# A macaron block as one stream of tile steps, with the state space stage spread over them

## The chip, the cores and the metric

The kernel runs on one core of one Trainium2 chip. The metric is the device time of one execution in microseconds (us). A core has five engines that work side by side, each strictly in the order of its own instructions: TensorE (PE, matmuls; its weight loads are shown apart as PEld), VectorE (DVE), ScalarE (ACT), GpSimd (POOL) and SyncE (SP), which here issues all transfers. They wait for one another by semaphores. SBUF is the working memory with 128 partitions; PSUM, with eight banks of 512 float32 per partition, takes TensorE's results.

## The reference, cut to what matters

x is 2048 tokens of 128 features. A transformer F of six layers is applied twice, with the same weights, around a state space layer S:

```python
x = x + 0.5 * F(layernorm(x))
x = x + S(layernorm(x))
x = x + 0.5 * F(layernorm(x))
...
# a layer of F; shift_tokens moves the upper half of the features by one token
x = attn_layer(shift_tokens(x), Wqkv[i], q_scale[i], k_scale[i], Wo[i]) + x
x = ffn_layer(shift_tokens(x), ln_g[i], ln_b[i], W1[i], b1[i], W2[i], b2[i]) + x
...
# in S: 256 channels with 16 states each, token after token
s = dA_t * s + dBu_t
y = jnp.einsum('bdn,bn->bd', s, C_t)
```

Attention is local: 16 heads of 64, windows of 32 tokens, and each window sees itself and the window before. The queries and keys are normalised and rotated. The feed-forward part has 341 hidden features and a gated GELU. So a token of F depends on tokens shortly before it, never on later ones, and S carries 256 x 16 states from the first token to the last.

## The kernel before, in words

All is float32, and the features lie on the partitions. The program has three stages one after the other: `transformer(k, xt, False)`, `state_space(k, xt)`, `transformer(k, xt, True)`.

**A transformer** runs over 6 x 16 tiles of 128 tokens. A tile's work is cut into some fifty short pieces, each on one engine. `run` loops over the steps i; in a step it goes through the list ORDER of (piece, lag) and emits piece by piece for tile i - lag. So the work of up to eight tiles stands interleaved in each engine's queue, in an order written out by hand (`manual_schedule`; SP is not in it). The pieces of a tile, with their lines:

- `project` (L263): queries and keys, two matmuls of 512 columns each; ScalarE squares them (L275), VectorE multiplies with cosines (L281) and sines (L287), GpSimd adds (L296), sums (L302) and a few short instructions give the norms, GpSimd scales (L328).
- `turn` (L341): 16 transposes; ScalarE copies them out (L350, L355).
- `score` (L378 masks, L389): 64 small matmuls; then copy (L400), maximum (L405), subtraction (L411), exponent (L417), sum (L422), division (L427), and a 32x32 transpose on VectorE (L437).
- `average` (L470): with the tile's inputs (transposed by L444, shifted by two copies between partitions on SP, L459 to L461) as weights, into two wide PSUM buffers z; ScalarE copies both into one tile zt of 4 x 16 x 32 columns (L482).
- `mix` (L490): the value and output weights were merged beforehand into one 128x128 matrix m per head. So the output of a tile is 16 matmuls, one per head, each with 128 columns (4 windows of 32), summed in one PSUM bank:

```python
for h in range(HEADS):
    self.nc.tensor.matmul(
        out=st.y_ps.rearrange("p (b q) -> p b q", q=WIN),
        lhsT=self.w[g // NT].m[:, h // 2, h % 2, :],
        rhs=st.zt[:, :, h, :],
```

- `residual` (L500) adds it to the stream r0 and writes r1.

Every fourth tile the feed-forward part follows for a block of 512 tokens: centring (L512), squares, variance (L534), reciprocal root, gates and values (L562), GELU (L581), product (L593), contraction (L606), residual (L617). Every layer's weights are loaded ahead by `load`; in the first pass `merge` (L207) forms m, and `biases` (L229) multiplies W1 with the bias of the norm: 12 records with one moving column.

PSUM is shared by three wide buffers of two banks (tag w: x_ps, t_ps, s_ps, z_ps and two thirds of g and a) and two narrow ones of one bank (tag n: the transposed inputs, centring, variance, mix, contraction, a third of g and a). A buffer goes to the next user in the order of the program; the writer waits until its last reader is done.

**The state space stage** is scheduled by the framework, not by hand. Per block of 512 tokens: two norms (L130, L88, L108, L120), projections (L772, L777), convolution (L783, L792), parameters (L803), and for the whole sequence the step sizes delta (L820 to L838). Then per block, state and channel half: TensorE spreads one row of B or C over the partitions (L851), ScalarE forms the decay (L856), VectorE multiplies (L860), scans along the tokens (L862) and multiplies with C (L868), and TensorE sums over the states with the identity (L869). All stages' edges are full stops: a stage begins when the one before has ended.

The whole program is shown below.

Of the kernel before, what the change touches and what calls it, by code (L numbers as in the profile page):

```python
# [56 lines left out]
PAD = WIN  # L57
NT = N // P
# [3 lines left out]
    ("FL", 1), ("XC", 5), ("PK", 0), ("XN", 6), ("NL", 1), ("XT", 2), ("SF", 5), ("T1K", 0),  # L62
    ("EZ1", 4), ("AQ", 1), ("NN", 1), ("S", 2), ("T2K", 0), ("MX", 2), ("EXW", 2), ("SK", 0),
    ("CQ", 1), ("V", 5), ("VE", 5), ("XD", 3), ("G", 6), ("PQ", 0), ("Y", 7), ("ES", 2),
    ("RQ", 1), ("DV", 3), ("GL", 6), ("CK", 1), ("UK", 0), ("EQ", 1), ("T1Q", 0), ("T2Q", 0),
    ("TP", 3), ("YR", 7), ("ZM", 4), ("SQ", 0), ("RK", 1), ("PX", 3), ("UQ", 0), ("EK", 1),
    ("SB", 2), ("EX", 2), ("A", 6), ("RS", 4), ("TB", 7), ("F1", 4), ("VT", 5), ("EZ0", 3),
    ("EP", 1), ("AK", 0), ("SM", 2), ("H", 6),
)

MANUAL = {ENG.PE, ENG.DVE, ENG.Activation, ENG.Pool}

# [5 lines left out]
def rstd_broadcast(k, sq, v, rb, sb):  # L78

    variances(k, sq, v)
    broadcast(k, powers(k, v, sb), rb)


def variances(k, sq, v):
    for j in range(4):
        k.nc.tensor.matmul(  # L88
            out=v[:, j : j + 1],
            lhsT=sq[:, bass.ts(j, P)],  # L90
            rhs=k.inv128,
            start=True,
            stop=True,
        )


def powers(k, v, sb):
    nc = k.nc
    ve = sb.tile([P, 4], F32, tag="ve", name="ve")
    nc.vector.tensor_scalar(ve, v[:, 0:4], LN_EPS, None, ALU.add)  # L100
    return diagonal(k, ve, sb)


def diagonal(k, ve, sb):

    nc = k.nc
    r = sb.tile([P, 4], F32, tag="r", name="r")
    nc.gpsimd.tensor_tensor(r, ve, k.nhalf.to_broadcast([P, 4]), ALU.pow)  # L108
    dg = sb.tile([P, 4, P], F32, tag="dg", name="dg", bufs=1)
    nc.gpsimd.tensor_tensor(  # L110
        dg,
        k.ident.unsqueeze(1).to_broadcast([P, 4, P]),
        r.unsqueeze(2).to_broadcast([P, 4, P]),
        ALU.mult,
    )
    return dg


def broadcast(k, dg, rb):
    k.nc.tensor.matmul(  # L120
        out=rb, lhsT=k.ones, rhs=dg.rearrange("p a b -> p (a b)"), start=True, stop=True
    )


def centred(k, src, ps, sb):


    nc = k.nc
    w_ps = ps.tile([P, 2, 512], F32, tag="w", name="w_ps")
    nc.tensor.matmul(out=w_ps[:, 0], lhsT=k.cen, rhs=src, start=True, stop=True)  # L130
    xc = sb.tile([P, HEADS, DH], F32, tag="sq", name="xc").rearrange("p h d -> p (h d)")[:, 0:512]
    nc.scalar.copy(xc, w_ps[:, 0])
    sq = sb.tile([P, 512], F32, tag="fsq", name="sq", bufs=1)
    nc.scalar.activation(sq, xc, AF.Square)
    rstd_broadcast(k, sq, w_ps[:, 0], w_ps[:, 1], sb)
    return xc, w_ps[:, 1]


def halves(at, n):


    return (slice(0, 64), bass.ds(PAD + at, n)), (slice(64, 128), bass.ds(PAD + at + 1, n))


class Transformer:
# [7 lines left out]
    def __init__(self, k, x, again, sb, wp, ps):  # L153
        self.k, self.nc, self.x, self.again = k, k.nc, x, again
        self.sb, self.wp, self.ps = sb, wp, ps
        self.at = [Ctx() for _ in range(DEPTH * NT)]
        for st in self.at:
            st.x, st.rot, st.sq, st.t2 = {}, {}, {}, {}
        self.ff = [Ctx() for _ in range(DEPTH * NB)]
        self.w = [Ctx() for _ in range(DEPTH)]  # L160
        self.tabs = {}
        self.r0 = wp.tile([P, PAD + N + 1], F32, tag="r0", name="r0", bufs=1)
        self.r1 = wp.tile([P, PAD + N + 1], F32, tag="r1", name="r1", bufs=1)

# [3 lines left out]
    def bank(self, name):  # L168
        return self.ps.tile([P, 512], F32, tag="n", name=name, bufs=2)
# [3 lines left out]
    def load(self, layer):  # L173
        nc, k, wp, w = self.nc, self.k, self.wp, self.w[layer]
        w.qk = wp.tile([P, 2 * INNER], F32, tag="qk", name="qk")
        nc.sync.dma_start(out=w.qk, in_=k.d_wqk[layer])
        if self.again:
            w.m = wp.tile([P, 8, 2, P], F32, tag="m", name="m")
            nc.sync.dma_start(out=w.m.rearrange("p c j f -> p (c j f)"), in_=k.merged[layer])
            return  # L180
        w.v = wp.tile([P, 8, P], F32, tag="wv", name="wv", bufs=1)
        nc.sync.dma_start(out=w.v, in_=k.d_wv[layer].rearrange("(c p) f -> p c f", p=P))
        w.o = wp.tile([P, 8, P], F32, tag="wo", name="wo", bufs=1)
        nc.sync.dma_start(out=w.o, in_=k.d_wo[layer].rearrange("(c p) f -> p c f", p=P))

    def load_ff(self, layer):
# [6 lines left out]
        )  # L193
        nc.sync.dma_start(out=w.w2[0:85, 2, :], in_=k.d_w2[layer, 256:FF])

    def merge(self, layer):

        nc, w = self.nc, self.w[layer]
        if self.again:
# [876 lines left out]
```

## Time and profile before

| | us |
|---|---|
| median of 3 runs | 3631.62 (3630.92 to 3637.47) |
| the profiled execution | 3634.36 |
| its span, first to last instruction | 3632.6 |
| first transformer | 0 to 1578 |
| state space stage | 1578 to 2079 |
| second transformer and output | 2079 to 3633 |

The profile page gives for each engine its busy time and its share of the span, then the span in 40 equal slices (each digit the busy share in tenths), the granted TensorE clock, the chain of work that ended last, and the costliest groups of instructions. A group's row has the line, the engine, the operation, output <- input by the program's names, shapes, the count, then the busy time in us, the mean ns of one, and the idle time before it with its releaser. Matmuls overlap, so a group's mean is the length of one record and not the distance from one to the next: that is read from the timeline, from one group's start to the next group's start. A float32 matmul shows as two records, each with a weight load of its own; a transpose is one.

### The profile page before, as it was taken

The page shows a single profiled execution, that of the slowest core. Times are in us where ns is not written, and L with a number is a line of the kernel's source. Part 1 is how long each engine was busy: PE and PEld are TensorE (multiplying, and loading weights), DVE is VectorE, ACT ScalarE, POOL GpSimd, SP SyncE. Part 2 cuts the span into 40 slices and gives each one's busy share as a digit, 9 for nine tenths or more (in the row PEclk, how much of TensorE's full clock was granted, in tenths as well). Part 3 has the DMA queues.
Part 4 walks back from the last instruction along what each step waited for, and adds up shares of the span by engine and source line. Part 5 has one row for each costly group of instructions (what it writes and reads, how often), then busy time and mean ns, then how long its engine had stood idle before and what let it go on. Part 6 is the DMA issues. An engine that isn't in the chain of part 4 may idle for free.

```text
span 3632.6 us, 93379 instructions
## 1 busy us (share of the span) xinstructions
PE 3453.6 (95%) x41200; PEld 2126.3 (59%) x41200; DVE 2818.5 (78%) x3188; ACT 2267.1 (62%) x3222; POOL 2767.5 (76%) x2182
## 2 busy tenths in 40 slices
PE   6999999999999999976999879999999999999997
PEld 3666666666666666632322346666666666666664
DVE  4778878888788878737988767888888888788884
ACT  3667676777767676734222267767676767676764
POOL 4989889899889899820100188999898989999993
PEclk7999999999999999976977889999999999999999
DMA  3010010100100000000000100010010100000000
GB/s 113 12 40 25 18 52 18 41 23 23 35 29 18 29 12 12 6 6 0 0 0 0 70 11 17 24 35 12 25 34 19 34 18 29 29 18 12 18 6 15
DMA packets 64892, 85.12 MB, mean 23 GB/s; under 512 B 8364, under 2 KB 53352, under 8 KB 61416
## 3 DMA queue, kind: packets, MB, share of 16 engines
q1 hardware_dynamic: 64488, 79.15, 7.0%
q8 instruction: 325, 5.32, 0.6%
q14 instruction: 79, 0.65, 0.1%
HBM read 59.39 MB, written 7.34 MB: 18 GB/s over the span
## 4 chain that ended last, share of the span: by engine, by line
PE 85%; DVE 4%; issue 4%; POOL 4%; ACT 3%; DMA 0%; POOLq 0%; SPq 0%; DVEq 0%; ACTq 0%
PE y_ps L490 19%; PE x_ps L263 18%; PE z_ps L470 10%; PE t_ps L341 9%; PE s_ps L389 7%; PE g_ps L562 4%; PE a_ps L562 4%; PE o_ps L606 3%; PE y L869 2%; DVE st L862 2%; PE s_ps L378 2%; PE c_ps L851 1%; PE v_ps L534 1%; PE c_ps L512 1%; PE b_ps L851 1%
## 5 line engine op out<-in xcount | busy, mean ns | idle before, releaser
L296 POOL TENSOR_TENSOR rot<-rot,t 128x1024 f32<-128x1024 f32 x384 | 906.9, 2362 | 18.4 <-DVE t L287 18.4
L263 PE MATMUL x_ps<-qk,r 128*128 128x512 f32 x1536 | 753.7, 614 | 11.1 <-ACT zt L482 8.8
L328 POOL TENSOR_TENSOR rot<-rot,rn 128x1024 f32<-128x1024 f32 x384 | 730.2, 1902 | 15.0
L490 PE MATMUL y_ps<-zt,m 128*128 128x128 f32 x6144 | 717.6, 275 | 4.0 <-ACT zt L482 4.0
L490 PEld LDWEIGHTS y_ps<-zt,m 128*128 128x128 f32 x6144 | 701.5, 192 | 7.7 <-ACT zt L482 5.7
L281 DVE TENSOR_TENSOR rot<-x_ps,tab 128x1024 f32<-128x1024 f32 x384 | 469.0, 1221 | 208.7 <-PE x_ps L263 208.6
L275 ACT ACTIVATE sq<-x_ps 128x1024 f32<-128x1024 f32 x384 | 394.4, 1027 | 323.7 <-DVE t L287 323.7
L302 DVE TENSOR_REDUCE ss<-sq 128x16 f32<-128x1024 f32 x384 | 468.4, 1220 | 79.0 <-ACT sq L275 76.8
L263 PEld LDWEIGHTS x_ps<-qk,r 128*128 128x128 f32 x1536 | 277.6, 192 | 368.0 <-issue 264.3
L287 DVE TENSOR_TENSOR t<-x_ps,tab 128x1024 f32<-128x1024 f32 x384 | 466.2, 1214 | 1.5 <-POOL rot L296 1.5
L341 PE MATMUL t_ps<-cs,rot 128*128 128x128 f32 x3072 | 406.9, 276 | 42.2 <-POOL rot L328 40.3
L341 PEld LDWEIGHTS t_ps<-cs,rot 128*128 128x128 f32 x3072 | 356.5, 143 | 154.5 <-issue 75.2
L422 DVE TENSOR_REDUCE rs<-pr 128x16 f32<-128x1024 f32 x192 | 234.2, 1220 | 248.8 <-ACT pr L417 248.6
L482 ACT COPY zt<-z_ps 128x1024 f32<-128x1024 f32 x384 | 385.0, 1004 | 22.8 <-PE z_ps L470 22.8
L470 PE MATMUL z_ps<-pt,xw 32*128 32x512 f32 x3072 | 388.1, 618 | 0.0
L411 POOL TENSOR_TENSOR pr<-pr,mx 128x1024 f32<-128x1024 f32 x192 | 365.2, 1902 | 22.7 <-ACT pr L400 22.7
L355 ACT COPY kt<-t_ps 128x1024 f32<-128x1024 f32 x192 | 194.5, 1013 | 296.8 <-PE t_ps L341 296.8
L427 POOL TENSOR_TENSOR pr<-pr,rs 128x1024 f32<-128x1024 f32 x192 | 365.1, 1901 | 12.4 <-DVE rs L423 12.4
L350 ACT COPY qt<-t_ps 128x1024 f32<-128x1024 f32 x192 | 194.5, 1013 | 159.8 <-PE t_ps L341 154.9
L389 PE MATMUL s_ps<-kt,qt 64*32 64x64 f32 x24576 | 288.7, 225 | 2.5 <-ACT kt L362 2.5
L389 PEld LDWEIGHTS s_ps<-kt,qt 64*32 64x32 f32 x24576 | 257.5, 105 | 48.9 <-ACT y L317 22.4
L856 ACT ACTIVATE da<-delta,a_neg 128x512 f32<-128x512 f32 x128 | 92.2, 722 | 256.2 <-DVE st L862 251.6
(142 smaller groups left out, 4604.5 us busy)
## 6 DMA issues: line engine op xcount, KB each, us to landing
tab<-in_tabs_dram SPq DMA_DIRECT2D x48, 512.0 KB, 3.6
qk<-in_wqk_dram SPq DMA_DIRECT2D x12, 1024.0 KB, 4.9
m<-m SPq DMA_DIRECT2D x12, 1024.0 KB, 11.8
xw<-xw SPq DMA_DIRECT2D x192, 48.0 KB, 2.6
w<-in_w_dram SPq DMA_DIRECT2D x12, 341.0 KB, 3.2
wv<-in_wv_dram SPq DMA_DIRECT2D x6, 512.0 KB, 4.1
wo<-in_wo_dram SPq DMA_DIRECT2D x6, 512.0 KB, 4.5
xw<-xw SPq DMA_DIRECT2D x180, 16.0 KB, 2.4
```

What stands on the lines that cost most here:

```text
L263: nc.tensor.matmul(out=x[:, j], lhsT=self.r0[:, bass.ds(PAD + g % NT * P, P)], rhs=self.w[g // NT].qk[:, bass.ds(kind * INNER + j * 512, 5 ...
L275: self.nc.scalar.activation(st.sq[kind], st.x[kind], AF.Square)
L281: self.nc.vector.tensor_tensor(st.rot[kind], st.x[kind], cos, ALU.mult)
L287: self.nc.vector.tensor_tensor(st.t2[kind].rearrange("p h (two c) -> p h two c", two=2), st.x[kind].rearrange("p h (two c) -> p h two c", ...
L296: self.nc.gpsimd.tensor_tensor(st.rot[kind], st.rot[kind], st.t2[kind], ALU.add)
L302: self.nc.vector.tensor_reduce(st.ss[:, kind, :], st.sq[kind], AX.X, ALU.add)
L328: self.nc.gpsimd.tensor_tensor(st.rot[kind], st.rot[kind], st.rn[:, kind, :].unsqueeze(2).to_broadcast([P, HEADS, DH]), ALU.mult,)
L341: self.nc.tensor.transpose(t_ps[:, c, :], flat[:, bass.ts(c, P)], self.k.ident)
L389: nc.tensor.matmul(out=st.s[32 * b : 32 * b + 32, par, c, :], lhsT=st.qt[rows, c, bass.ts(b, WIN)], rhs=st.kt[rows, c, bass.ds(WIN * b, 2 ...
L470: self.nc.tensor.matmul(out=st.z[b // 2][:, b % 2].rearrange("p (h q) -> p h q", q=WIN), lhsT=st.xw[rows, j, :], rhs=st.pt[rows, :, j, :], ...
L482: self.nc.scalar.copy(st.zt[:, 2 * half : 2 * half + 2].rearrange("p b h q -> p b (h q)"), st.z[half])
L490: self.nc.tensor.matmul(out=st.y_ps.rearrange("p (b q) -> p b q", q=WIN), lhsT=self.w[g // NT].m[:, h // 2, h % 2, :], rhs=st.zt[:, :, h, ...
```

## The change

The program becomes one stream of 192 tile steps. Both passes run in two segments of 1024 tokens (8 tiles): pass one segment 0 through all six layers, then segment 1, then pass two segment 0, then segment 1. What a segment's first tile needs of the segment before (last keys, last inputs, one column of r0 and r1) is kept, in DRAM or in small tiles. The state space layer works on blocks of 256 tokens; the blocks of segment 0 run in the steps of pass one's segment 1, those of segment 1 in the steps of pass two's segment 0. A block gets ten steps; in eight of them (`STATES`) two of its 16 states are done, so 64 of the 192 steps have state work. ORDER now holds a position within the step for every piece, and pieces that are not in it are put in by `at_time`; `room` looks for a stretch in which the narrow PSUM buffer is free by these positions.

Other things differ with it. The feed-forward part works on 256 tokens (every second tile). zt is now two tiles, one per half, in three buffers, and `mix` runs per half. The narrow PSUM buffer is single; one bank holds the sum over the states. B and C are written to DRAM and spread by a broadcasting load, so L851's matmuls go. The decays lie in a wide PSUM buffer, and the scan runs in place there. The norms' reciprocal roots use ScalarE and VectorE as in the feed-forward part. The rotation tables and W1, once scaled, are kept in DRAM for later segments and passes. The blocks after a state space layer re-enter r0 by `enter`. Output leaves per 256 tokens (`result`).

```diff
 ORDER = (
-    ("FL", 1), ("XC", 5), ("PK", 0), ("XN", 6), ("NL", 1), ("XT", 2), ("SF", 5), ("T1K", 0),
...
+    ("EQ", 2, 0.032), ("Y", 7, 0.046), ("UK", 1, 0.050), ("PX", 4, 0.064), ("VE", 6, 0.065),
+    ("YR", 7, 0.098), ("PQ", 0, 0.099), ("SM", 3, 0.125), ("VT", 6, 0.129), ("AK", 1, 0.144),
...
+    ("CK", 1, 0.475), ("ZM", 4, 0.511), ("GL", 6, 0.543), ("SS", 0, 0.548), ("A", 6, 0.601),
+    ("T2K", 0, 0.613), ("T1K", 0, 0.646), ("RS", 4, 0.679), ("SB", 2, 0.689), ("H", 6, 0.695),
+    ("DA", 0, 0.776), ("AQ", 0, 0.798), ("SF", 5, 0.814), ("EX", 2, 0.838), ("YA", 1, 0.864),
+    ("RK", 1, 0.866), ("EK", 1, 0.867), ("SC", 0, 0.875), ("RQ", 1, 0.876), ("CP", 0, 0.879),
+    ("V", 5, 0.900), ("XD", 2, 0.949),
+STATES = (0, 1, 2, 3, 5, 6, 7, 8)
+ROUND = 10
...
     def bank(self, name):
-        return self.ps.tile([P, 512], F32, tag="n", name=name, bufs=2)
+        return self.ps.tile([P, 512], F32, tag="n", name=name, bufs=1)
...
     def averages_out(self, g, half):
         st = self.at[g]
         if half == 0:
-            st.zt = self.sb.tile([P, 4, HEADS, WIN], F32, tag="zt", name="zt")
-        self.nc.scalar.copy(
-            st.zt[:, 2 * half : 2 * half + 2].rearrange("p b h q -> p b (h q)"), st.z[half]
-        )
+            st.zt = [None, None]
+        st.zt[half] = self.sb.tile([P, 2, HEADS, WIN], F32, tag="zt", name="zt", bufs=3)
+        self.nc.scalar.copy(st.zt[half].rearrange("p b h q -> p b (h q)"), st.z[half])

     def mix(self, g):
         st = self.at[g]
         st.y_ps = self.bank("y_ps")[:, 0:P]
-        for h in range(HEADS):
-            self.nc.tensor.matmul(
-                out=st.y_ps.rearrange("p (b q) -> p b q", q=WIN),
-                lhsT=self.w[g // NT].m[:, h // 2, h % 2, :],
-                rhs=st.zt[:, :, h, :],
-                start=(h == 0),
-                stop=(h == HEADS - 1),
-            )
+        for half in range(2):
+            for h in range(HEADS):
+                self.nc.tensor.matmul(
+                    out=st.y_ps[:, bass.ts(half, 64)].rearrange("p (b q) -> p b q", q=WIN),
+                    lhsT=st.w.m[:, h // 2, h % 2, :],
+                    rhs=st.zt[half][:, :, h, :],
+                    start=(h == 0),
+                    stop=(h == HEADS - 1),
+                )
...
     def hidden(self, f, at, name):
-        two = self.bank2(name)
-        out = [two[:, 0], two[:, 1], self.bank(name)]
+        out = self.bank2(name).rearrange("p j (m t) -> p (j m) t", t=SUB)
...
+    def broadcast(self, s, q):
+        b = self.sub[s]
+        bc = self.sp.tile([P, 2, 2, SUB], F32, tag="bc", name="bc", bufs=2)
+        rows = self.k.bc[s].rearrange("(k n) t -> k n t", k=2)[:, 2 * q : 2 * q + 2, :]
+        self.nc.sync.dma_start(out=bc, in_=rows.partition_broadcast(P))
+    def source(self, s, q):
...
+        for j in range(2):
+            self.nc.gpsimd.tensor_tensor(
+                b.s[:, j], bs[:, j].unsqueeze(1).to_broadcast([P, 2, SUB]), b.du, ALU.mult
+            )
+    def decay(self, s, q):
+        b.da = self.bank2("da").rearrange("p j (c t) -> p j c t", c=2)
...
+                self.nc.scalar.activation(
+                    b.da[:, j, c], b.d[:, c], AF.Exp, scale=self.a_neg[:, c, n : n + 1]
+                )
+    def scan(self, s, q):
...
+                nc.vector.tensor_tensor_scan(
+                    b.da[:, j, c],
+                    b.da[:, j, c],
+                    b.s[:, j, c],
+                    self.carry[:, c, n : n + 1],
...
+    def observe(self, s, q):
+        nc.vector.tensor_copy(
+            self.carry[:, :, 2 * q : 2 * q + 2].rearrange("p c j -> p j c"),
+            b.da[:, :, :, SUB - 1],
+        )
...
+        nc.vector.tensor_tensor(
+            b.sc, b.da, cs.unsqueeze(2).to_broadcast([P, 2, 2, SUB]), ALU.mult
+        )
+    def gather(self, s, q):
...
+        for j in range(2):
+            self.nc.tensor.matmul(
+                out=b.y_ps.rearrange("p c t -> p (c t)"),
+                lhsT=self.k.ident,
+                rhs=b.sc[:, j].rearrange("p c t -> p (c t)"),
...
+    def segments(self, sp):
+        self.open_space(sp)
+        for s in range(8):
+            seg, j = divmod(s, 4)
+            leaves = (seg * DEPTH + DEPTH) * ST + 2 * j + 0.25
+            self.space(s, max(leaves, self.base + ROUND - LEAD))
...
+        for i in range(-2, TILES + last + 2):
...
+            todo = [(pos, self.stage, (i, name, lag)) for name, lag, pos in ORDER]
+            for _, f, args in sorted(todo + self.todo.pop(i, []), key=lambda x: x[0]):
+                f(*args)
...
-    transformer(k, xt, False)
-    state_space(k, xt)
-    transformer(k, xt, True)
```

`space` emits the other pieces of a block of 256 tokens in its ten steps: two norms, the projections, the convolution, the parameters, the step sizes on GpSimd and ScalarE, and behind the last state the gated output, its contraction, the sum with the stream and `enter`.

## Prediction

> **What bounds the kernel now.** I read the page first (engines, slices, chain), then a table of windows that cuts the span into stages, then the same table for the instruction of L444, which runs once per tile, and last the timeline of TensorE in the middle of a stage. The page:
>
> ```profile
> span 3632.6 us, 93379 instructions
> PE 3453.6 (95%) x41200; PEld 2126.3 (59%) x41200; DVE 2818.5 (78%) x3188; ACT 2267.1 (62%) x3222; POOL 2767.5 (76%) x2182
> PE   6999999999999999976999879999999999999997
> ...
> PEclk7999999999999999976977889999999999999999
> ...
> PE 85%; DVE 4%; issue 4%; POOL 4%; ACT 3%; DMA 0%; POOLq 0%; SPq 0%; DVEq 0%; ACTq 0%
> ...
> L490 PE MATMUL y_ps<-zt,m 128*128 128x128 f32 x6144 | 717.6, 275 | 4.0 <-ACT zt L482 4.0
> L490 PEld LDWEIGHTS y_ps<-zt,m 128*128 128x128 f32 x6144 | 701.5, 192 | 7.7 <-ACT zt L482 5.7
> ```
>
> TensorE is busy 95% of the span and holds 85% of the chain. Slices 18 to 24 are another regime: there the granted clock falls to 0.6 to 0.8 (one slice aside). The group to remember is the mix, L490: its weight loads are busy 701.5 us, almost as long as its matmuls. The windows, first of all engines, then of L444 alone:
>
> ```profile
> core 0: us, PE busy (x) PEld busy (x) DVE busy (x) ACT busy (x) POOL busy (x), PEclk, DMA share, GB/s
> 300.00:1292.00 992.00, 991.13 (x13522) 652.84 (x13521) 798.25 (x886) 696.28 (x998) 896.11 (x679) 1.00 0.09 27
> ...
> 1578.00:2079.00 501.00, 425.32 (x746) 147.24 (x746) 392.54 (x496) 145.07 (x198) 60.41 (x127) 0.76 0.04 14
> ```
>
> ```profile
> 300.00:1292.00 992.00, 17.45 (x64) 9.05 (x64) 1.00 0.09 27
> ```
>
> In 992 us 64 tiles pass, 15.50 us each, and TensorE is busy in 991.1 of them at full clock. Per tile VectorE has 12.5 us of work, ScalarE 10.9, GpSimd 14.0. So a transformer step costs what TensorE does in it, to the last half per cent; the other engines have 1.5 us or more to spare. The state space stage lasts 501 us (1578 to 2079) at clock 0.76. The whole: 96 x 15.5 = 1488 of the first 1578 us, so 90 us of start, fill and drain; 501; 1554 - 1488 = 66 us of fill, drain and output. I sum against the profiled execution, 3634.4 us with 1.8 us around its span; the median of the runs shown, 3631.6, is 0.1% below it.
>
> **Mix in two halves (the decisive term).** L490 now issues 16 matmuls per tile with 128 moving columns. Afterwards each half tile has a tile of its own, and there are 32 matmuls with 64 moving columns; in the built program's order the count is 6144 in place of 3072. Each float32 matmul is two records, each with its own load of 128x128 weights. What does a record with half the columns cost? The timeline (start, duration, engine, line):
>
> ```profile
> 1016.90 3.74 PE L490 MATMUL y_ps<-zt,m 128*128 128x128 f32 x32
> 1020.47 1.04 PE L341 MATMUL t_ps<-cs,rot 128*128 128x128 f32 x8
> ...
> 1024.33 1.25 PE L229 MATMUL b_ps<-pv,w 128*128 128x1 f32 x12
> 1025.44 1.96 PE L263 MATMUL x_ps<-qk,r 128*128 128x512 f32 x4
> ```
>
> ```profile
> 1024.33 1.16 PEld L229 LDWEIGHTS b_ps<-pv,w 128*128 128x128 f32 x11 [0.24 <-issue]
> 1025.41 0.30 PEld L263 LDWEIGHTS x_ps<-qk,r 128*128 128x128 f32 x2
> ```
>
> The mix starts at 1016.90 and the next group at 1020.47: 3.57 us for 32 records, 111.6 ns each. L229 moves one column only, and its 11 loads still take 1025.41 - 1024.33 = 1.08 us. Seven of them have 128 columns of weights and four have 85 (L229's third chunk): 1236 columns, 0.874 ns each, 112 ns for a full load. With 1 moving column and with 128 the price of a record is thus the same: the load sets it. A record with 64 lies between the two, so 64 x 111.6 ns = 7.14 us per tile, 3.57 more; x 192 = **+685 us**, all on the bounding engine. The low end is the bare mean of L229, 1.08 / 11 = 98 ns: +2.71 us, +520. The high end is the 117 ns of 3.74 us / 32: +750. I take 685, because the bare mean holds the narrow loads.
>
> The Trainium skill, "TensorE: Matmul & The Clock Gate", Back-to-back issue gap, puts the distance of matmuls at moving columns / 2.4 + 2.5 ns, about 25 ns for 1 to 64 columns; by it alone halving would be free and the sum below 685 us lower. The row speaks against it: 112 ns with one column. The same page's section LDWEIGHTS has columns of weights / 1.2, an estimate of 107 ns here, 6.83 us per tile and a sum 60 us lower than mine.
>
> **Feed-forward in blocks of 256.** In the same timeline a block of 512 costs from start to next start: g 2.68, a 2.68, o 2.58, centring and variance 0.96 each: 9.86. A record of 512 columns takes 0.427, so a group carries 0.02 to 0.12 that doesn't shrink. With 256: 1.40 + 1.40 + 1.30 + 0.53 + 0.53 = 5.16 per pair of tiles, +0.115 per tile, **+22 us** (0 to 60). On other engines the second half of a split costs about 0.15 us fixed (128x1024 1.22 us, 128x512 0.69), and ScalarE's table loads (1.28 us, L581 and L689) double, 0.64 us per tile. VectorE goes to about 12.8, ScalarE to 12, beside a TensorE step of 15.50 + 3.57 + 0.12 = 19.2: hidden. If the mix weren't dearer, GpSimd would have that cover thin.
>
> **State space in the steps.** The 501 us go. On TensorE come 64 groups that sum the states (4 records of 0.43 plus 0.11: 1.82 us), 116 us; and per 256 tokens 15 matmuls of 256 columns (30 records of 0.213) in ten groups (0.11 each), 7.5 us, x 8 = 60. **+176 us**, now at full clock. The 128 matmuls of L851 become 64 broadcast loads of 0.5 MB on SP; the nearest row is the table load, 512 KB in 3.6 us, and they are issued 0.9 step (some 17 us) ahead. Behind them in SP's queue stand the copies of xw, needed over a step later. GpSimd gets two 128x512 products per state step (1.27 us each by L554) and some 11 us per 256 tokens: 14.0 + 2.5 + 1.1 = 17.6 us in a step of 19.2 + 1.8 + 0.75; hidden.
>
> A new wait: the decays lie in one of the three wide PSUM buffers, and the next step's z_ps takes that buffer. In VectorE's order the scans and the product stand behind the residual, which waits for the mix. After the mix of an even step TensorE has the state sum, 16 turns and a variance: 1.82 + 1.85 + 0.53 = 4.2 us. VectorE has the residual 0.8, four scans (half of 1.27 each, 2.6), the copy 0.2 and a 128x1024 product 1.22, with handoffs 5.0. Behind an odd step it is 6.4 against 7.1, as h waits for a. So TensorE waits about 0.8 us in 64 steps: **+51 us** (0, if the scans come early, to 160). Queued behind z_ps is all of TensorE.
>
> The narrow PSUM buffer is single now. In each step the holders (xw, centring, variance, mix, output) have other TensorE work between them that is longer than the copy out; only the state space's extra ones stand close. By the order there are some 9 per 256 tokens, each behind a residual or copy of 0.3 to 0.8 us: 72 x 0.5 = **+36 us** (0 to 150, the latter one residual's 0.8 us in each of 192 steps).
>
> **Edges.** One start, fill and drain instead of two. Today the first x is turned at 9.5 us and the first projection stands at 44; with blocks of 256 normalised one by one I count 9.5 + about 8 us of short instructions before it, then the 46 us of fill and drain that the first stage has, then some 10 of output: **75 us** (50 to 110) in place of 90 + 66. Eight blocks must re-enter for the second pass; by the schedule each does so 7 steps or more before its first projection, so no wait there. Merges and biases are inside 15.50.
>
> **Sum.** 2976 (192 x 15.50) + 685 + 22 + 176 + 51 + 36 + 75 = 4021, and 1.8 around the span: **4023 us**, 10.7% slower. What is won (501 + 81 of edges - 176 - waits) is 320; what is lost on the mix is 685.
>
> **Rivals.**
> 1. *The mix stays at 3.57 us* (loads run ahead better when the matmuls are short). For it: only that no row has 64 columns with full weights. Against it: the rows on both sides. Then 4023 - 685 = 3338, but a state step of 15.6 + 2.6 = 18.2 us is as long as GpSimd's 17.6, and up to 2 us x 64 come back: 3340 to 3470, say 3390, faster by 7%. It decides from where the loss of 389 us is gone: 389 / (192 x 64) = 32 ns less per record, so a record of 64 columns below some 80 ns.
> 2. *The single narrow buffer binds in every step.* For it: five pairs of users on one bank, TensorE strictly in order. Against: the work between them, above. 0.8 us x 192 = 154 in place of 36: 4141, and as much again per extra holder in the state steps (some 40 us): 4180.
> 3. *The overlap fails*: a block's chain runs past its ten steps, and TensorE waits at each handoff. The stage's 501 less its 176 would come back: 4350. The schedule's slack speaks against it.
>
> **Chances.** Forecast 0.80, first rival 0.09, second 0.09, third 0.02. The range runs from the low price of the mix alone (4023 - 165) to the upper ends of both waits in part: 3860 to 4160. A measurement of this kernel tells 0.2% from no change; faster 0.09, same 0.01, slower 0.90.
>
> **What would show it.** The mix group (now line 587) with 12288 records at 7.1 us per tile, its loads busy without gaps; steps of 19.2 us without state work and about 21.8 with it; TensorE over 95% busy at clock 1.0 throughout; idle time ahead of z_ps put down to the product of L1025. I am wrong if the mix takes under 6 us per tile, or if VectorE or GpSimd carry the chain.

## The result, and the profile after

The changed kernel takes **4268.5 us** (median of 4 runs, 4259.2 to 4272.5), the kernel before 3631.3 on the same chip: ratio 1.177, 95% interval 1.170 to 1.183. The forecast was 4023 with a range up to 4160: right in sign, 245 us too low. The profiled execution took 4272.0, its span 4270.2.

In the changed kernel the mix is L587, the residual behind it L603, the queries' and keys' projection L350, z_ps L567, the key copy kt L442, the feed-forward residual L722. Of the state space, the variance of its norms is L316 (with its root on ScalarE, L276), the decays L997, the scans L1007, the product with C L1025, and the sum over states L1035. The page of the changed kernel:

```profile
span 4270.2 us, 109734 instructions
PE 4019.0 (94%) x48080; PEld 2985.7 (70%) x48080; DVE 2829.7 (66%) x3578; ACT 2523.0 (59%) x3985; POOL 2948.6 (69%) x2413
PE   6999999998999999999999898989999999999998
...
PEclk9999999998999999999999999999999999999998
...
PE 80%; DVE 9%; ACT 6%; POOL 3%; issue 2%; SPq 0%; DMA 0%; DVEq 0%; POOLq 0%; ACTq 0%
...
L587 PE MATMUL y_ps<-zt,m 128*128 128x64 f32 x12288 | 1409.8, 276 | 8.8 <-ACT xc L633 3.3
```

The separate regime in the middle is gone, as it should be, and the mix's busy time has doubled from 717.6 to 1409.8 us. But the digit 8 stands now and then in TensorE's row, and VectorE's share of the chain rose from 4% to 9%. The windows of the changed kernel, first a stretch in which state steps run and one without, then L539 alone (one record per tile: its count is the number of tiles):

```profile
1000.00:3000.00 2000.00, 1838.72 (x20893) 1332.66 (x20889) 1377.06 (x1790) 1183.68 (x1910) 1403.37 (x1149) 0.96 0.16 43
3700.00:4200.00 500.00, 497.22 (x6557) 380.67 (x6561) 333.32 (x406) 309.24 (x475) 353.07 (x281) 1.00 0.08 22
```

```profile
1000.00:3000.00 2000.00, 24.92 (x83) 12.01 (x83) 0.96 0.16 43
3700.00:4200.00 500.00, 7.11 (x26) 3.66 (x26) 1.00 0.08 22
```

Without state work a tile takes 500 / 26 = 19.2 us, TensorE is busy 99% at full clock: what was forecast. With it, 2000 / 83 = 24.1 us in place of 21.8, TensorE is busy 92%, and the clock is 0.96. So most of the miss lies in the state steps. TensorE's timeline there (start, duration, idle time before and its releaser):

```profile
1618.76 2.40 PE L587 MATMUL y_ps<-zt,m 128*128 128x64 f32 x20
1621.93 0.67 PE L316 MATMUL v_ps<-sq,ones 128*128 128x256 f32 x2 [0.77 <-DVE r L603]
1622.44 1.88 PE L1035 MATMUL y_ps<-sc,cs 128*128 128x512 f32 x4
1624.16 1.91 PE L428 MATMUL t_ps<-cs,rot 128*128 128x128 f32 x16
1626.30 0.70 PE L644 MATMUL v_ps<-sq,ones 128*128 128x256 f32 x2 [0.23 <-ACT sq L638]
1628.14 4.58 PE L567 MATMUL z_ps<-pt,xw 32*128 32x512 f32 x16 [1.14 <-ACT kt L442]
1632.66 3.65 PE L350 MATMUL x_ps<-qk,r 128*128 128x512 f32 x4
```

and the same two groups where no state work runs:

```profile
3922.10 7.25 PE L587 MATMUL y_ps<-zt,m 128*128 128x64 f32 x64
3929.19 1.92 PE L428 MATMUL t_ps<-cs,rot 128*128 128x128 f32 x16
...
3931.47 2.00 PE L567 MATMUL z_ps<-pt,xw 32*128 32x512 f32 x16
3933.40 1.98 PE L350 MATMUL x_ps<-qk,r 128*128 128x512 f32 x4
```

Three short waits, 2.14 us together, and then z_ps takes 4.58 us in place of 2.00 and x_ps 3.65 in place of 1.98: the granted clock is 0.50 from 1630 to 1636 us. 2.14 us of waits bring 4.3 us more behind them, about 3.4 of them by some 7 us at half clock. What TensorE waits for in the changed kernel (us in total, times, longest):

```profile
PE x_ps L350 <- DVE r L722: 36.3, 27, 2.5
PE s_ps L473 <- ACT zt L580: 19.7, 16, 1.5
PE z_ps L567 <- ACT kt L442: 18.5, 17, 1.4
PE i_ps L539 <- DVE q L286: 17.2, 10, 2.4
PE v_ps L316 <- DVE r L603: 15.5, 20, 0.8
PE c_ps L622 <- ACT xw L546: 14.3, 15, 2.9
```

No single one is large: they name both VectorE and ScalarE, and users of the narrow PSUM buffer (i_ps, v_ps, c_ps). The wait that the prediction named, z_ps for the product, has 3.5 us.

### The profile page after: what moved, and what is told of

It is laid out like the page before. It is cut to its first block, busy times and chain, and to the rows that moved or that the text cites. A ratio compares the mean times of both kernels' runs of the same rounds, so it can differ in the third digit from the quotient of the medians.

```text
span 4270.2 us, 109734 instructions
## 1 busy us (share of the span) xinstructions
PE 4019.0 (94%) x48080; PEld 2985.7 (70%) x48080; DVE 2829.7 (66%) x3578; ACT 2523.0 (59%) x3985; POOL 2948.6 (69%) x2413
## 4 chain that ended last, share of the span: by engine, by line
PE 80%; DVE 9%; ACT 6%; POOL 3%; issue 2%; SPq 0%; DMA 0%; DVEq 0%; POOLq 0%; ACTq 0%
PE y_ps L587 31%; PE x_ps L350 16%; PE z_ps L567 7%; PE t_ps L428 6%; PE s_ps L484 5%; PE g_ps L664 3%; PE a_ps L664 3%; DVE da L1007 2%; PE o_ps L708 2%; PE c_ps L622 1%; DVE sc L1025 1%; PE y_ps L1035 1%; PE s_ps L473 1%; DVE ss L389 1%; ACT zt L580 1%
## 5 line engine op out<-in xcount | busy, mean ns | idle before, releaser
L587 PEld LDWEIGHTS y_ps<-zt,m 128*128 128x128 f32 x12288 | 1417.7, 194 | 66.3 <-ACT xc L633 30.9
L587 PE MATMUL y_ps<-zt,m 128*128 128x64 f32 x12288 | 1409.8, 276 | 8.8 <-ACT xc L633 3.3
L383 POOL TENSOR_TENSOR rot<-rot,t 128x1024 f32<-128x1024 f32 x384 | 900.7, 2359 | 7.5 <-DVE rot L368 4.8
L350 PE MATMUL x_ps<-qk,r 128*128 128x512 f32 x1536 | 792.8, 641 | 50.6 <-DVE r L722 36.3
L603 DVE TENSOR_TENSOR r<-y_ps,r 64x128 f32<-64x128 f32 x384 | 111.0, 289 | 756.0 <-PE y_ps L587 753.4
L350 PEld LDWEIGHTS x_ps<-qk,r 128*128 128x128 f32 x1536 | 281.4, 198 | 413.5 <-issue 246.9
L442 ACT COPY kt<-t_ps 128x1024 f32<-128x1024 f32 x192 | 193.7, 1009 | 482.4 <-PE t_ps L428 482.4
L567 PE MATMUL z_ps<-pt,xw 32*128 32x512 f32 x3072 | 441.2, 634 | 22.1 <-ACT kt L442 18.5
L396 POOL TENSOR_SCALAR ss<-ss 128x32 f32<-128x32 f32 x192 | 54.8, 285 | 477.5 <-DVE ss L389 473.0
L428 PE MATMUL t_ps<-cs,rot 128*128 128x128 f32 x3072 | 374.7, 276 | 3.5 <-POOL rot L415 2.3
L512 ACT ACTIVATE pr<-pr 128x1024 f32<-128x1024 f32 x192 | 202.1, 1053 | 205.9 <-POOL pr L506 205.2
L567 PEld LDWEIGHTS z_ps<-pt,xw 32*128 32x128 f32 x3072 | 160.3, 187 | 201.2 <-issue 129.8
```

The costliest lines, as they stand in the source:

```text
L350: nc.tensor.matmul(out=x[:, j], lhsT=self.columns(g), rhs=st.w.qk[:, bass.ds(kind * INNER + j * 512, 512)], start=True, stop=True,)
L383: self.nc.gpsimd.tensor_tensor(st.rot[kind], st.rot[kind], st.t2[kind], ALU.add)
L428: self.nc.tensor.transpose(t_ps[:, c, :], flat[:, bass.ts(c, P)], self.k.ident)
L567: self.nc.tensor.matmul(out=st.z[b // 2][:, b % 2].rearrange("p (h q) -> p h q", q=WIN), lhsT=st.xw[rows, j, :], rhs=st.pt[rows, :, j, :], ...
L587: self.nc.tensor.matmul(out=st.y_ps[:, bass.ts(half, 64)].rearrange("p (b q) -> p b q", q=WIN), lhsT=st.w.m[:, h // 2, h % 2, :], rhs=st.z ...
```

## The experiments

Theories: **A**, ScalarE stands at the root of the state space's norms (L276), whose variance TensorE reaches only behind the mix, and the single narrow buffer does the rest. **B**, VectorE does scans and product behind the mix's residual, and TensorE's next group waits for it. The price of the mix had to be checked apart from both. Each ratio stands against the kernel before on the same chip, which itself ran between 3598 and 3645 us there; differences between two kernels are those of their medians.

### The mix alone

**b_mix_halves**: the kernel before with nothing but the mix in halves.

```diff
+for half in range(2):
     for h in range(HEADS):
         self.nc.tensor.matmul(
-            out=st.y_ps.rearrange("p (b q) -> p b q", q=WIN),
+            out=st.y_ps[:, bass.ts(half, 64)].rearrange("p (b q) -> p b q", q=WIN),
...
-            rhs=st.zt[:, :, h, :],
+            rhs=st.zt[:, 2 * half : 2 * half + 2, h, :],
```

> The kernel before with one part of the change alone: the mix in two halves of 64 columns, 32 matmuls in place of 16. Theory (a record costs its weight load of 112 ns whatever it moves): 3.57 us more per tile on the bounding engine, 3631 + 685 = 4316, between 4280 and 4340. Rival (a record follows its moving columns, and the lost time lies elsewhere): 3631 to 3660.

4297.0 us, ratio 1.189 (1.181 to 1.196), before 3618.2: +679 (655 to 711 by the interval). The mix group of this kernel:

```profile
L491 PE MATMUL y_ps<-zt,m 128*128 128x64 f32 x12288 | 1398.1, 275 | 2.2 <-ACT zt L482 2.2
```

A record of 64 columns has a mean of 275 ns, as one of 128 had before, and there are twice as many. One edit alone makes the old kernel as slow as the new one.

**a_mix_whole**: the changed kernel with the mix undivided, both halves in one tile zt (a single buffer, in place of three of half the size).

```diff
-for half in range(2):
     for h in range(HEADS):
...
-            rhs=st.zt[half][:, :, h, :],
+            rhs=st.zt[:, :, h, :],
```

> The changed kernel with the mix undivided (one zt tile, 16 matmuls of 128 columns). Theory: 4268 - 685 = 3583, up to 100 more since waits that stood in the shadow of a longer step come out: 3580 to 3690, so about as fast as the kernel before. Rival (the steps with state work are bound by VectorE and GpSimd by now, TensorE only waits): 3800 or more.

3624.7 us, ratio 1.001 (0.998 to 1.004): 644 less, level with the kernel before. So with the mix undivided the rest of the change neither wins nor loses. Its steps without state work take 500 / 32 = 15.6 us, those with it 800 / 38 = 21.05, 3.2 above the 17.8 of TensorE's work. Its waits:

```profile
PE z_ps L567 <- ACT kt L442: 55.4, 40, 4.4
PE x_ps L350 <- DVE r L722: 42.8, 29, 1.9
```

### Where the state space's time goes

**a_no_space** leaves the state space layer out; the blocks still re-enter by `enter`.

```diff
+self.base = int(max(np.ceil(time + 4.5), self.base + ROUND))
+self.enter(s, self.base + 11.2, sp)
+return
```

> The changed kernel without the state space layer (a block re-enters the second pass as it left the first; the whole layer is left out of the computation). Theory (the 245 us by which the forecast was short lie in the steps with state work): 192 x 19.2 = 3686 and 75 to 100 of edges and the first layer's steps, 3750 to 3800. Rival (they lie in every step, from the single narrow PSUM buffer, or in the edges): 3950 to 4010.

3837.4 us, ratio 1.062, above the theory's range and far below the rival's: the layer costs 4268.5 - 3837.4 = 431 us, 176 of which are TensorE's work by the prediction's count; 255 are not. Tiles of this kernel in its windows:

```profile
0.00:500.00 500.00, 6.61 (x23) 3.23 (x23) 0.96 0.24 75
500.00:1000.00 500.00, 7.17 (x26) 3.66 (x26) 0.99 0.13 38
1000.00:1500.00 500.00, 7.20 (x26) 3.66 (x26) 1.00 0.12 36
...
3500.00:3836.00 336.00, 3.84 (x14) 1.97 (x14) 0.95 0.05 14
```

Three tiles are missing in the first 500 us and, at 19.2 us each, three and a half in the last 336. The span is 3836.2, and 3836.2 - 3683 (192 of the forecast's steps of 19.18) = 153 are edges.

**a_states_only** has the sums over states and all that feeds them, with constant step sizes, inputs, B and C in place of the pieces (norms, projections, convolution, gated output).

```diff
-time = self.layernorm(s, time, sp, normal)
...
-self.enter(s, time + 0.4, sp)
+at(base - 0.1, stand_in)
+self.enter(s, base + 11.2, sp)
```

> The changed kernel with the 64 state steps, but without the pieces around them (the norms, projections, convolution, step sizes and output of the state space layer are left out; the states are fed with constants and rows of x). Without all of the layer 3837 us, with all of it 4268: 431, of which 176 are TensorE's work. Theory A (the other 255 come mostly from the pieces: ScalarE stands at a variance that TensorE reaches only behind the mix, and the single narrow buffer is handed on late): 3837 + 116 + 50 to 100 = 4000 to 4050. Theory B (they come from VectorE's scans behind the mix): 3837 + 116 + 180 to 220 = 4130 to 4170.

4078.0 us, ratio 1.126: 241 above a_no_space, 116 of work and 125 of waits.

**a_pieces_only** has the pieces and no states; the gated output takes a product in place of their sum.

```diff
-self.states[base + step] = s, q
-at(base + step - 0.9, self.broadcast, s, q)
+pass
```

> The changed kernel with the pieces of the state space layer but without its 64 state steps (the scans, decays and sums over states are left out; the output takes delta times u in place of the sum). Theory A (the pieces cause the waits): 3837 + 60 + 130 to 180 = 4030 to 4080. Theory B (the state steps cause them): 3837 + 60 + 20 to 60 = 3920 to 3960.

4073.7 us, ratio 1.125: 236, of which 60 work and 176 waits. Separately the waits are 125 + 176 = 301, together 255: both theories are alive.

### Changes of order

**a_scan_early** puts decays, scans and product ahead of the residual. With its single product buffer a sum takes the product of its own step and not of the step before, so it computes wrong sums; its work is the same.

```diff
-    ("DA", 0, 0.776), ("AQ", 0, 0.798), ("SF", 5, 0.814), ("EX", 2, 0.838), ("YA", 1, 0.864),
-    ("RK", 1, 0.866), ("EK", 1, 0.867), ("SC", 0, 0.875), ("RQ", 1, 0.876), ("CP", 0, 0.879),
+    ("DA", 0, 0.545), ("AQ", 0, 0.798), ("SF", 5, 0.814), ("EX", 2, 0.838), ("YA", 1, 0.864),
+    ("RK", 1, 0.866), ("EK", 1, 0.867), ("SC", 0, 0.660), ("RQ", 1, 0.876), ("CP", 0, 0.661),
```

> The changed kernel with the decays, scans and the product put ahead of the residual in the order of ScalarE and VectorE, so that VectorE does them while TensorE is in the mix. Theory (TensorE waits behind VectorE's state work that begins only after the mix, and runs at half clock after each wait): 100 to 180 us less, 4090 to 4170. Rival (the waits come from the extra users of the narrow buffer): 4230 to 4270.

4325.3 us, 57 more than the changed kernel, since each sum now waited for its own step's product (94.4 us). **a_scan_early3** mends that with two product buffers, taken in turn by the pairs of states.

```diff
+sc = self.sp.tile([P, 2, 2, SUB], F32, tag="sc", name="sc", bufs=2)
+setattr(b, f"sc{q}", sc)
...
-st.zt[half] = self.sb.tile([P, 2, HEADS, WIN], F32, tag="zt", name="zt", bufs=3)
+st.zt[half] = self.sb.tile([P, 2, HEADS, WIN], F32, tag="zt", name="zt")
```

> The changed kernel with decays, scans and product of the states issued ahead of the mix's residual on VectorE (at .545, .660, .661 of a step), each pair of states with its own product buffer, so that the step after sums the right product; two zt tiles in place of three pay for it. All of the computation is done. Theory B (TensorE's waits in the state space steps come from VectorE doing scan and product behind the residual, though it is idle during the divided mix): 50 to 120 us less than the changed kernel's 4268, so 4150 to 4220. Theory A (they come from ScalarE standing at the state space's variances and narrow PSUM pieces): within 25 us of 4268. Slower than 4300 would say that the residual, not the scan, is what TensorE needs next.

4246.7 us, ratio 1.171 (1.165 to 1.177): 22 less, not 50 to 120. That is within theory A's 25, and the interval overlaps the changed kernel's (1.170 to 1.183), so even the 22 are not sure. The wait of x_ps for L722 is gone from the head of its list, and in its place stand

```profile
PE v_ps L316 <- DVE r L603: 24.1, 20, 1.6
PE o_ps L924 <- DVE r L603: 20.1, 6, 3.4
PE x_ps L852 <- DVE r L603: 20.0, 8, 3.3
```

The residual has become late. **a_var_odd** moves the two variance groups of a block ahead of the mix.

```diff
-time = self.room(time, 0.19)
+if time > DEPTH * ST:
+    odd = 2 * np.floor(time / 2) + 1.306
+    time = odd if time <= odd else odd + 2
+    self.taken.append((time, time + 0.19))
+else:
+    time = self.room(time, 0.19)
```

> The changed kernel with the state space's two variance groups moved ahead of the mix (to the odd steps, right behind the turns of x), so that ScalarE does not stand at their root while TensorE does the mix. All of the computation is done. Theory A: ScalarE's 180 us ahead of the root mostly go, and with them 50 to 120 us of the time, with fewer microseconds at half clock: 4150 to 4220. Theory B: within 25 us of 4268.

4340.4 us, 72 more. ScalarE's idle time ahead of the root did go (from 182.5 us behind L316 to 31.4), but now these wait:

```profile
PE x_ps L355 <- DVE r L727: 40.4, 27, 2.2
PE y_ps L592 <- DVE q L286: 24.9, 22, 1.2
PE c_ps L627 <- ACT xw L551: 20.5, 20, 2.5
...
PE v_ps L316 <- ACT xw L551: 17.4, 24, 2.7
```

The wait of x_ps for the feed-forward residual stood in the changed kernel too (36.3 us). The other three are users of the narrow buffer that stand behind one another. The same kind of move was tried with the undivided mix, against a_mix_whole's 3625: **w_sums_late** puts the key sums behind the feed-forward residual on VectorE.

```diff
-("UK", 1, 0.050)
+("UK", 1, 0.1)
```

> The mix undivided, and on VectorE the sums of squares of the key behind the feed-forward residual instead of ahead of it. The queries' matmuls of every second step wait for that residual, 43 us in 29 waits in the kernel with the undivided mix (3625). If these waits are on the chain: 20 to 60 us less with the half clock that follows them, 3565 to 3605. Rival (another wait takes their place): 3615 to 3635.

3632.7 us, ratio 1.004: nothing won. **w_scan_early** adds the early scans and the product buffers of a_scan_early3 to it.

> As the kernel with late sums, and the decays, scans and product ahead of the mix's residual on ScalarE and VectorE, with two buffers for the product, so that a step's sum over states uses the product of the step before, as in the changed kernel. Theory B (the scans behind the mix cause the waits): 60 to 150 us less than with late sums alone, about 3430 to 3530. Theory A (the pieces do): within 30 us of it, 3550 to 3620.

3865.8 us, ratio 1.068, against both theories: here VectorE is idle for only 64 us ahead of the residuals (in a_scan_early3, with the longer mix, for 518), and v_ps waits 66.6 us for them. **w_var_odd** has a_var_odd's edit, **w_exp_late** puts the exponentials behind the key copy on ScalarE:

```diff
-("EX", 2, 0.838)
+("EX", 2, 0.8675)
```

> The same move of the variance groups, with the mix undivided (one zt tile, 128 columns; against 3625 for the undivided mix alone). Theory A: the state steps of 21 us come down by 0.5 to 1.5 us, so 30 to 100 us less: 3525 to 3595. Theory B: 3610 to 3640.

> The undivided mix, with the exponentials of the state space issued on ScalarE behind the copy of the keys' product in place of ahead of it: of the undivided mix alone, the largest wait of TensorE was z_ps for the key copy kt, 55 us in 40 waits. If that wait is ScalarE's order, it goes, and the time falls by 30 to 80 us with what it costs in clock: 3545 to 3595. If the wait only moves (as it did when the key sums were put later on VectorE), 3610 to 3640.

3625.1 us (ratio 0.999, 0.997 to 1.002) and 3636.8 (1.002, 0.999 to 1.004). With the exponentials late, z_ps no longer waits for the key copy but 25.9 us for the product. **w_both** joins these two edits.

> Undivided mix with both moves, the variance groups ahead of the mix and the exponentials behind the key copy; nothing is left out. Each alone left the time within 12 us of 3625. If the waits are separate and add up, 3580 to 3610, below both kernels; if a wait taken away is given back at the next handoff, 3615 to 3645.

3620.9 us, ratio 0.999 (0.995 to 1.002). No order tried beats the kernel before by more than its interval.

### Loads taken away

Orders only passed waits on, so the loads were tried. **s_no_scan** is a_states_only without the scans.

```diff
-nc.vector.tensor_tensor_scan(
-    b.da[:, j, c],
-    b.da[:, j, c],
-    b.s[:, j, c],
...
+pass
```

> State steps only (4078 us, of which 125 us in 64 steps are neither TensorE work of the sums nor the kernel without state space), with the four scans of each state step left out too: the product takes the decays as they are, 3.0 us of VectorE less per state step. If VectorE's work behind the residual is what TensorE waits for, 80 to 125 us go: 3955 to 4000. If another engine or the order of the pieces is, 4055 to 4085.

3958.8 us: 119 of the 125 us are gone. The broadcast loads, GpSimd's products and ScalarE's decays are all still in this kernel, so together they cost no more than the 6 us that are left. **s_no_decay** leaves ScalarE's decays out, and the scans read the step sizes.

> State steps only, with ScalarE's four decays of each state step left out: the scans read the step sizes in their place, 1.9 us of ScalarE less per state step, and no wait of VectorE for ScalarE there. If ScalarE's work or that handoff is what TensorE waits for, 80 to 125 us go: 3955 to 4000. If VectorE's own work is, 4055 to 4085.

4173.9 us, 96 *more*, which neither theory expected. The scan's group shows why, first in a_states_only, then here:

```profile
L992 DVE TENSOR_TENSOR_SCAN da<-da,carry,s 128x256 f32<-128x256 f32 x256 | 193.5, 756 | 18.9 <-ACT da L982 6.5 <-DVE da L992 0.5
```

```profile
L990 DVE TENSOR_TENSOR_SCAN da<-d,carry,s 128x256 f32<-128x256 f32 x256 | 289.0, 1129 | 12.4 <-DVE da L990 0.5
```

The scans took 95.5 us more of VectorE in all, and the time rose by 96. But 1129 ns is a mean of two kinds of scan. By line, with the shortest, median and longest time in ns, again first in a_states_only, then here:

```profile
L992 DVE TENSOR_TENSOR_SCAN da<-da,carry,s x256: 743/757/760, 1082.6 to 2980.1; 128x256 f32<-128x256 f32 x128
```

```profile
L990 DVE TENSOR_TENSOR_SCAN da<-d,carry,s x256: 745/759/2893, 1079.6 to 3070.4; 128x256 f32<-128x256 f32 x128
```

Here both operands of the scan lie in SBUF, and 81 of the 256 scans took 0.96 to 2.9 us. Every one of these 81 began while GpSimd was in an addition or product of its own (L383 in 69 cases, L333 in 12) and ended 0.55 us after that had ended; they account for 94.5 of the 95.5 us. One step of the timeline, four scans beside two additions:

```profile
1100.42 6.51 DVE L990 TENSOR_TENSOR_SCAN da<-d,carry,s 128x256 f32<-128x256 f32 x4
```

```profile
1099.66 5.06 POOL L383 TENSOR_TENSOR rot<-rot,t 128x1024 f32<-128x1024 f32 x2
```

In a_states_only, with the first operand in PSUM, 159 scans ran beside L383 as well, and none took over 0.76 us. So the extra time is waiting for GpSimd, and it holds VectorE's queue like work. If it passes into the time one for one, ScalarE's relief of 1.9 us a step won nothing; the two were not separated. By these two runs VectorE's time in a state step passes into the whole about one for one once it is late (+95.5 gave +96), and taking it away wins until the 125 us are used up (193.5 less gave 119). The idle time ahead of x_ps goes with it, in a_states_only and in s_no_scan:

```profile
L350 PE MATMUL x_ps<-qk,r 128*128 128x512 f32 x1536 | 773.4, 627 | 47.2 <-DVE r L722 41.9 <-DVE sc L1010 2.9 <-ACT mst L227 2.1
```

```profile
L350 PE MATMUL x_ps<-qk,r 128*128 128x512 f32 x1536 | 759.0, 617 | 2.1 <-ACT mst L227 2.1
```

**p_two_narrow** gives a_pieces_only a second narrow buffer, in the bank that the sum over states doesn't use there.

```diff
-return self.ps.tile([P, 512], F32, tag="n", name=name, bufs=1)
+return self.ps.tile([P, 512], F32, tag="n", name=name, bufs=2)
```

> Pieces only (4074 us, of which 176 us are neither TensorE work of the pieces nor the kernel without state space), with two narrow PSUM buffers in place of one, as the bank of the sum over states is not used there. If the single narrow buffer makes the waits, as its term in the sum says (36 us) or its rival (150 us), 36 to 150 us go: 3925 to 4040. If ScalarE's order at the pieces makes them, 4055 to 4085.

3985.0 us: 89 of the 176 are gone. **p_narrow_var** adds the move of a_var_odd, which alone had failed.

> Pieces only, with two narrow PSUM buffers (3985 us) and the variance groups moved ahead of the mix. 3985 is 88 us above the 3897 of the kernel without state space plus the 60 us of TensorE work of the pieces. If ScalarE standing at the root while TensorE does the mix makes these 88 us, and the move alone (a_var_odd) failed because it met the other holders of the single narrow buffer, 40 to 90 us go: 3895 to 3945. If neither, within 15 us of 3985 or above.

3894.5 us: another 90 gone, and with 3837.4 + 60 = 3897 no more waits are left than without the layer (TensorE idle 94.5 us, in a_no_space 95.2). No run has the move in the pieces alone with a single narrow buffer, so that it needed the second one is argued from a_var_odd. ScalarE's idle time ahead of the root, in a_pieces_only, p_two_narrow and p_narrow_var:

```profile
L276 ACT ACTIVATE rs<-v_ps,eps 128x256 f32<-128x256 f32 x128 | 62.0, 484 | 192.2 <-PE v_ps L316 176.7 <-PE v_ps L644 15.5
```

```profile
L276 ACT ACTIVATE rs<-v_ps,eps 128x256 f32<-128x256 f32 x128 | 62.1, 485 | 149.9 <-PE v_ps L316 142.8 <-PE v_ps L644 7.1
```

```profile
L276 ACT ACTIVATE rs<-v_ps,eps 128x256 f32<-128x256 f32 x128 | 62.3, 486 | 33.9 <-PE v_ps L316 26.8 <-PE v_ps L649 7.1
```

What TensorE waited for there were mostly ScalarE's copies zt, which come after the root in its queue. In p_two_narrow:

```profile
PE x_ps L350 <- ACT zt L580: 48.9, 19, 3.8
PE s_ps L473 <- ACT zt L580: 42.6, 22, 2.2
```

In p_narrow_var these two waits are 0.7 and 17.1 us; a new one, z_ps for the key copy, has 20.0.

**w_no_scan** leaves the scans out of a_mix_whole, by the edit of s_no_scan.

> The undivided mix (3625 us) with the scans of all state steps left out. If VectorE's work behind the residual sets the state steps there too, at one microsecond for one as in the divided kernel, 3.0 us x 64 = 193 us at most and 80 at least go: 3430 to 3545. If the waits on the key copy and on the pieces set them, 3580 to 3630.

3531.9 us: 93 less, about half of the 193 us of scans. VectorE's work counts there too, though the largest wait by the list was the key copy's; that one fell from 55.4 to 26.9 us, though neither the copy nor its place in ScalarE's order was changed.

## Why the prediction was wrong in size

From the runs: 3837 (a_no_space) + 176 of work + 125 (states) + 176 (pieces) - 46 (waits shared when both run) = 4268. Against the forecast's 4021 this is 247 more: 168 in the waits (51 + 36 = 87 forecast, 255 found) and 78 in the edges (75 forecast, 153 found). So three terms of the sum were too small, the wait behind the scans, the narrow buffer and the edges, and a fourth, ScalarE at the variance, was missing.

- **The mix: right.** Forecast +685; +679 put in alone, 644 taken out of the changed kernel (TensorE's idle time then rises from 251 to 300 us: the longer mix had covered some waits). In the trace 3929.19 - 3922.10 = 7.09 us per tile, forecast 7.14. The prediction held a formula of the Trainium skill ("TensorE: Matmul & The Clock Gate", Back-to-back issue gap: columns / 2.4 + 2.5 ns) against its row, by which halving would be free. The section gives that formula for an isolated matmul and says that in a stream of weight loads and matmuls both set the distance and that the formula counts too little at small sizes. So it was no rule against the row, and b_mix_halves shows the 679 us. The estimate from the page's section LDWEIGHTS gave 60 us less than mine, and the runs are nearer to the row.
- **Steps and feed-forward: right.** 19.2 us without state work, as forecast. The 22 us of feed-forward blocks and the 176 us of TensorE's state work were not measured apart; with p_narrow_var within 3 us of 3837 + 60, the latter's 60 at least fits.
- **The waits behind the scans: the mechanism right, the size and the place wrong.** The prediction had VectorE 0.8 us late in each of 64 steps, 51 us; 125 were measured, 1.95 a step, and 119 went with the scans. The failed step is "four scans (half of 1.27 each, 2.6)": 256 columns took 0.756 us, not 0.635, which is 0.5 us a step, 31 of the 74 us that were missing. The rest I had not counted: VectorE, once late, is late for what follows in its queue, and x_ps waits for the feed-forward residual L722 (36.3 us) rather than z_ps for the product (3.5).
- **The single narrow buffer: too small.** Forecast 36; 89 went with a second buffer, in the pieces alone; in the whole kernel it was not tried. I had priced each of its extra holders by a copy of 0.5 us; that TensorE's delay also brings the half clock was in no term.
- **ScalarE at the variance: missing.** No term of the sum stood for it; 90 us (p_narrow_var, in the pieces alone). The prediction asked what a *writer* of the buffer waits for, and not what is queued on ScalarE behind a root whose variance TensorE reaches only after 7 us of mix: the copies zt, for which TensorE then waits.
- **The clock: wrong.** "Clock 1.0 throughout" was forecast. The mean is 0.970 over 4270.2 us against 0.989 over 3836.2 without state space: 127 - 42 = 85 us of full speed lost. With 156 us more of idle TensorE this is 241 of the 255; 14 us stay unexplained.
- **Edges: too small.** 75 forecast, 153 found: the first 500 us of a_no_space hold 23 tiles in place of 26, the last 336 hold 14 in place of 17.5. Which handoffs of the fill and the drain take it was not tried.
- **Rivals.** The cheap mix fell. The narrow buffer binding in *every* step fell too (19.2 us where no state runs), though it did in the steps that have pieces. Of the third, that the overlap fails and 325 us come back, 255 did, but the list of waits shows none for a block that ran past its steps: the waits are within the steps.

What stays open: why the waits overlap by 46 us, and whether two narrow buffers and fewer scans would carry the undivided mix below 3620; the banks of PSUM are all in use, so this wasn't tried.

## What to carry to other kernels

A record's price for a shape that the trace lacks can be bracketed by rows on either side of it: that term held to 1% in the trace (7.09 us against 7.14). When work is put into the gaps of a schedule, it is not an engine's total load that decides but what it has to do between the last input it gets and the next group of the bounding engine, and, on an in-order engine, how long an instruction that waits blocks the rest. If changes of order only move a wait, take a load away: that is what told the three causes apart here, and it also showed a move that cost 72 us in the whole kernel and won 90 in the pieces alone with the narrow buffer doubled. And a mean can hide two kinds of instruction: look at its shortest and longest before reading a price from it.

## What the runs showed of the hardware

- **The clock falls after short waits.** In the records of the changed kernel the clock changes in steps of 3.41 us. Of 942 such stretches at full clock with under 0.1 us of TensorE idle none was followed by half clock; with 0.1 to 1.0 us idle 5 of 135 were, with 1.0 to 1.4 us 8 of 46, with 1.4 to 2.0 us 16 of 27, above that all 16. The Trainium skill, "TensorE: Matmul & The Clock Gate", Why this matters for your kernels, warns of gaps above some 3 us; here 1.4 to 2.9 us in one stretch, in one piece or in two, were often enough.
- **A scan with both operands in SBUF waits for GpSimd.** In s_no_decay 81 of 256 scans of 256 columns took 0.96 to 2.9 us, each until 0.55 us after the end of a GpSimd addition or product of SBUF tiles that was running when it began; the median was 759 ns. With the first operand in PSUM the median was 757 ns and the longest 761, in the changed kernel too, where 152 of its 256 scans ran beside L383. So there the decays in PSUM kept the scans clear of GpSimd. In the kernel before, 512 columns all in SBUF took 1274 ns.
